# Causal attention over 32 keys in a perceiver kernel: values copied onto the diagonal of standing buffers, row sums as a column of ones, one key product, and both 32-key stages in written order

## The chip, the cores and the metric

The kernel runs on one core of one Trainium2 chip. The metric is the device time of one execution in microseconds. Five engines work side by side: PE (TensorE, matrix products), DVE (VectorE), ACT (ScalarE), POOL (GpSimd) and SP (SyncE, which issues transfers). Operands lie in SBUF, matrix products go to PSUM, which has eight banks of 512 float words for each of 128 partitions. PEld is the loading of PE's weights, which runs beside the products.

## The reference

The input x has 64 sequences of 32 tokens of 256 numbers; the context has 64 × 257 rows of 64 numbers. Six residual steps follow each other, each on a layer norm of x:

```python
x = x + _L0_xattn_ref(_layernorm(x), ctx_512, ...)   # A: 16 heads of 16, causal
x = x + _L0_attn_ref(_layernorm(x), ...)             # B: 16 heads of 128, shared key and value
x = x + _L0_ffn_ref(_layernorm(x), ...)              # C: the best 4 of 16 blocks
x = x + _L1_xattn_ref(_layernorm(x), ctx_512, ...)   # D: 16 heads over 257 rotated keys
x = x + _L1_attn_ref(_layernorm(x), ...)             # E: 16 heads of 16, causal, 4 key groups
x = x + _L1_ffn_ref(_layernorm(x), ...)              # F: 8 experts, the best one of them
```

The change is in A and E. The core of E (A is the same with 16 own key and value heads, without biases, and with an output product; only the first 32 of its keys are seen, since the mask is causal and there are 32 queries):

```python
q = jnp.einsum('bse,hed->bhsd', x, Wq) + bq[None, :, None, :]
kg = jnp.einsum('bse,ged->bgsd', x, Wk) + bk[None, :, None, :]
vg = jnp.einsum('bse,ged->bgsd', x, Wv) + bv[None, :, None, :]
k = jnp.repeat(kg, per, axis=1)      # each key group serves 4 heads
v = jnp.repeat(vg, per, axis=1)
scores = jnp.einsum('bhqd,bhkd->bhqk', q, k) * (1.0 / np.sqrt(d))
scores = jnp.where(causal[None, None, :, :], -jnp.inf, scores)
attn = jax.nn.softmax(scores, axis=-1)
out = jnp.einsum('bhqk,bhkd->bhqd', attn, v)
```

## The kernel before, in words

**Tiling.** The 2048 tokens are 16 tiles of 128 (four sequences of 32 each), which stay in SBUF as xs[t] for all six stages. Four tiles make a group: layer norms, their transposes (PE, then a copy by ACT) and the query and key products are made for a group of 512 tokens at a time; scores, softmax and outputs for a tile. The stages follow one another in one program: A (L335–487), B, C, D (to L1465), E (L1470–1703), F.

**A tile of a 32-key stage.** `scores` (L264) multiplies 32×32 blocks: 64 small matmuls give 16 heads of 32 queries × 32 keys for each of the four sequences, in a PSUM tile of four banks, of which the first 128 columns of each are used. `softmax_rows` (L211) is a chain over three engines: DVE scales and masks (L216), DVE takes the maximum (L225), POOL subtracts it (L226), ACT takes the exponential (L227), DVE sums (L229) and takes the reciprocal (L231). `heads_on_partitions` (L234) transposes the result on PE (L239) and ACT copies it to SBUF (L241), so that 4 heads × 32 keys lie on the partitions. `gather` multiplies by a block-diagonal matrix vd of the values: for each sequence j and each four heads c a matrix of 128 × 64, zero except where a row's head is the column's head.

**The values.** In A, `values` (L402) makes them with PE in two "mm" tiles (L410), and four DVE multiplications by the mask m4 write vd, zeros included (L420). In E, inside `score`, PE makes v in an "mm" tile (L1501), DVE adds the bias (vbe, L1509), and four POOL multiplications by m4 write vd (L1512), in a rotating set of three buffers. The "mm" tiles are two buffers that the transposes, the query and key products, the values and the router share.

**Normalising.** In A, POOL multiplies the exponentials by the reciprocal sums before the transpose (L399). In E, DVE multiplies the gathered output by them (L1532), and POOL adds it to x (L1538).

**The features of E.** `e_features` (L1158) makes q of a group (part 1; two column halves o) and the keys (part 2). For the keys, each half o is a product of its own (L1162) and two ACT steps with a 0/1 mask write kd (L1175), whose two halves hold the same keys.

**D's second half** also prepares E. A table of steps (L1349–1362), run one by one between D's products, holds for E the norms of groups 0 and 1 (steps 48 and 61), the start of group 0 (50), and its transposes, query and key products (51, 55, 56, 58, 59, 60).

**Routing in E.** F sends each token to one expert, so E also makes, as soon as tiles are done, their norm statistics (`route_stats`, DVE L152–153), the norm (`route_norm`: POOL copies L1551, the power on POOL, ACT L1558, more POOL copies), its transpose (`route_turn`, L1571, L1574), the router's product and argmax (`route`, L1583–1606, a chain of DVE steps that ends in oh and cum), and the ranks and the scattered rows (`send`, rank L1613, L1616, POOL's indirect transfers L1629). A table `routing` names the tile at which each runs: one group's four steps at t = 5–8, 9–12, 13–16, the last tiles' at 15 to 17.

**What sets the order.** The program's instructions are ordered for each engine by the framework's scheduler, except on the engines that a block lists in `manual_schedule(engines=...)`: there the written order stands. In A and in E only PE is listed. The loops of the two stages write it down:

```python
for t in range(NT + 2):                       # A, L470-487
    score(t + 1); project(t - 2); values(t + 1)
    turned[t] = heads_on_partitions(...); gather(t - 1)
    group(t // 4 + 1, t % 4)                  # norm and transposes of the next group at part 0
    for step in first.get(t, ()): step()      # B's first norms and keys, at t = 9 to 15
```

In E (L1680–1698) the order is score(t+1) with its values, heads of t, the features of the next group (for t > 1), gather(t−1), its route statistics, routing. In A the norm of the next group stands in part 0 of `group`, right ahead of its transposes; in E in part 3, a tile earlier.

Of the kernel before, what the change touches and what calls it, by code (L numbers as in the profile page):

```python
# [7 lines left out]
F32 = mybir.dt.float32  # L8
AF = mybir.ActivationFunctionType
ALU = mybir.AluOpType  # L10
# [35 lines left out]
def perceiver_kernel(ctx: ExitStack, tc: tile.TileContext, a: dict, out: bass.AP):  # L46
# [107 lines left out]

    def ln_group(g, name, twice=False, act=False, power=False):

        mv = sm(f"lnm_{name}{g}", [P, 4, 2])
        for i in range(4):
            stats(mv[:, i, :], xs[4 * g + i], f"{name}{g}_{i}")
        rs = rstd_of(mv, 4, f"{name}{g}", power)  # L160
        if twice:

            v2 = sm(f"lnw_{name}{g}", [P, 4, 2])
            nc.vector.tensor_tensor(v2[:, :, 1], mv[:, :, 1], rs, ALU.mult)
            nc.vector.tensor_tensor(v2[:, :, 1], v2[:, :, 1], rs, ALU.mult)
            rs2 = rstd_of(v2, 4, f"{name}{g}b", power)
            nc.vector.tensor_tensor(rs2, rs2, rs, ALU.mult)
            rs = rs2
        sh = sm(f"lnh_{name}{g}", [P, 4])
        nc.vector.scalar_tensor_tensor(sh, mv[:, :, 0], -1.0, rs, ALU.mult, ALU.mult)  # L170
        xn = []
        for i in range(4):
            y = xnp.tile([P, D], F32, tag="xn", name=f"xn_{name}{g}_{i}")
            x_ = xs[4 * g + i]
            if act:
                nc.scalar.activation(
                    y, x_, AF.Identity, scale=rs[:, i : i + 1], bias=sh[:, i : i + 1]
                )
            else:
                nc.vector.scalar_tensor_tensor(  # L180
                    y,
                    x_,
                    rs[:, i : i + 1],
                    sh[:, i : i + 1].to_broadcast([P, D]),
                    ALU.mult,
                    ALU.add,
                )
            xn.append(y)
        return xn
# [22 lines left out]
    def softmax_rows(s_ps, t, work, name):  # L212
# [14 lines left out]
        nc.scalar.activation(s, s, AF.Exp)  # L227
        su = sm(f"su_{name}{t}", [P, NH])
        nc.vector.tensor_reduce(su, s, AX.X, ALU.add)  # L229
        ri = sm(f"ri_{name}{t}", [P, NH])  # L230
        nc.vector.reciprocal(ri, su)  # L231
        return s, ri
# [31 lines left out]
    def scores(ps, qT, kd, i, name):  # L264

        s_ps = ps.tile([P, 4, 512], F32, tag="S", name=f"S_{name}")
        for o in range(KC):
            for j in range(4):
                for r in range(4):
# [4 lines left out]
                        kd[rs, o, 4 * i + j].rearrange("p w k -> p (w k)"),  # L274
# [61 lines left out]
    with tc.tile_pool(name="wA", bufs=2) as work, tc.tile_pool(  # L336
# [3 lines left out]
    ) as ps2, tc.manual_schedule(engines={mybir.EngineType.PE}):  # L340
# [15 lines left out]
        def group(g, part):  # L356
# [7 lines left out]
            if part == 0:  # L364
                feats[g][2] = transposed(ln_group(g, "a", power=True), ps2, g, "a")
# [27 lines left out]
        def score(t):  # L393
            g, i = divmod(t, 4)
            qT, kd, _ = feats[g]
            s_ps = scores(ps1, qT, kd, i, f"a{t}")
            sc[t] = softmax_rows(s_ps, t, work, "a")
            s, ri = sc[t]
# [57 lines left out]
        for _ in range(18):  # L456
            nc.tensor.matmul(warm, pad[:, 0:P], pad[:, 0:256], start=True, stop=True)
        for part in (0, 1, 2):
            group(0, part)
        score(0)  # L460
        values(0)

# [7 lines left out]
        for t in range(NT + 2):  # L470
# [8 lines left out]
            if t < NT:  # L479
                turned[t] = heads_on_partitions(sc.pop(t)[0], ps1, t, work, "a")  # L480
            if 1 <= t <= NT:
                gather(t - 1)
            group(t // 4 + 1, t % 4)
            for step in first.get(t, ()):
                step()
# [651 lines left out]
    with mbw, wd1:  # L1137
# [3 lines left out]
        with tc.tile_pool(name="wD", bufs=2) as work, tc.tile_pool(  # L1141
# [7 lines left out]

            def e_group_start(g):  # L1150
                feats[g] = (
                    e_w.tile([P, KC, 512], F32, tag="qT", name=f"qTe{g}"),
                    e_w.tile([P, KC, 16, 2, S], F32, tag="kd", name=f"kde{g}"),
# [3 lines left out]
            def e_features(g, part, o, ps):  # L1157

                qT, kd, xT = feats[g]
                q_ps = ps.tile([P, 512], F32, tag="mm", name=f"qe{g}_{o}_{part}")  # L1160
# [193 lines left out]
            steps[48] = lambda: lat.update(e=ln_group(0, "e", power=True))  # L1354
# [535 lines left out]
```

## Time and profile before

| what | value |
|---|---|
| runs | 1299.14, 1298.5 and 1304.86 us; median 1299.14 |
| the profiled execution's own time | 1298.15 us |
| its span, from first to last instruction | 1296.4 us |
| mean granted clock of PE, as a share of full | 0.943 |
| busy, share of the span: PE, DVE, ACT, POOL | 92%, 59%, 42%, 30% |
| instructions | 26028 |

The stages lie one after the other in the span: A to about 151 us, B and C after it, D from 660 to 992, E from 992 to about 1149, F to the end. Two windows of the trace, one of A and one of E, show what each engine did there. The columns are the window, its length, the busy time (and number of instructions) of PE, PEld, DVE, ACT and POOL, the granted clock, the share of the DMA engines in use, and GB/s:

```profile
18.00:145.00 127.00, 104.57 (x2194) 65.55 (x2196) 79.51 (x205) 51.98 (x102) 39.47 (x41) 0.89 0.66 208
1062.00:1072.00 10.00, 6.11 (x168) 5.05 (x168) 8.21 (x26) 1.64 (x4) 7.36 (x21) 0.57 0.01 2
```

In the views of groups, a line names the code line, the engine, the operation, output <- inputs and the shape of a kind of instruction, how often it ran, its busy time in us and the mean ns of one, and behind the last bar the idle time of its engine just before it and what ended it. A group can be busy for less than its number times its mean, since matmuls overlap. A releaser in square brackets in an order of time is the same for one instruction.

### The profile page before, as it was taken

What the parts mean: (1) busy time and instruction counts of PE and PEld (TensorE: products, weight loads), DVE (VectorE), ACT (ScalarE), POOL (GpSimd) and SP (SyncE); (2) the same over time, 40 slices, a digit from 0 to 9 for tenths busy, and PEclk for the clock granted to TensorE, in tenths of its full rate; (3) what the DMA queues carried; (4) which work ended last, traced back from release to release, by engine and by line L of the source; (5) the groups of instructions that cost most, each with busy time, mean ns of one, the idle gap of its engine ahead of it and who ended that gap; (6) DMA issues with size and microseconds to landing.
All of it is one profiled execution on the core that took longest, in us unless ns stands there. A gap on an engine that the chain in (4) does not pass through costs nothing. (4 is left out here: it accounts for less than half of the span.)

```text
span 1296.4 us, 26028 instructions
## 1 busy us (share of the span) xinstructions
PE 1187.8 (92%) x10189; PEld 833.3 (64%) x10189; DVE 769.0 (59%) x1751; ACT 540.1 (42%) x1255; POOL 389.7 (30%) x504
## 2 busy tenths in 40 slices
PE   6898999999999999999989999999998687669997
PEld 4555767767767566777756767777766455536664
DVE  5665345778758865533288877777674574334432
ACT  2336354554544641222365656556563233211111
POOL 2232251554524631000055252000002577621111
PEclk8889999999999989979999989999999788669999
DMA  7991110111021220912154353111103700011110
GB/s 232 309 332 36 28 42 1 41 42 41 25 83 42 59 65 2 283 33 68 44 149 131 62 143 93 46 35 48 34 1 127 266 3 19 22 50 42 43 39 18
DMA packets 94588, 103.10 MB, mean 80 GB/s; under 512 B 37664, under 2 KB 71201, under 8 KB 93986
## 3 DMA queue, kind: packets, MB, share of 16 engines
q1 hardware_dynamic: 92594, 97.19, 25.8%
q0 software_dynamic: 1872, 4.23, 0.9%
q8 instruction: 82, 1.34, 0.4%
q14 instruction: 40, 0.33, 0.1%
HBM read 69.45 MB, written 32.85 MB: 79 GB/s over the span
## 5 line engine op out<-in xcount | busy, mean ns | idle before, releaser
L1261 ACT ACTIVATE pp<-Sd,nm 128x257 f32<-128x257 f32 x256 | 118.2, 475 | 71.9 <-DVE nm L1257 66.1
L706 PE MATMUL qb<-xT_b,b_q 128*128 128x256 f32 x512 | 123.0, 389 | 0.0
L706 PEld LDWEIGHTS qb<-xT_b,b_q 128*128 128x128 f32 x512 | 95.6, 191 | 39.5 <-issue 19.6
L797 PE MATMUL yb<-b_o,oTb 128*128 128x256 f32 x512 | 116.1, 386 | 0.0
L797 PEld LDWEIGHTS yb<-b_o,oTb 128*128 128x128 f32 x512 | 98.4, 194 | 14.3 <-issue 1.0
L1270 DVE TENSOR_TENSOR pp<-pp,rd 128x514 f32<-128x514 f32 x128 | 98.4, 769 | 2.1
L1257 DVE TENSOR_REDUCE nm<-Sd 128x2 f32<-128x514 f32 x128 | 83.0, 685 | 19.2 <-PE Sd L1249 19.0
L1292 ACT COPY pTd<-pt 128x512 f32<-128x512 f32 x112 | 61.5, 599 | 52.1 <-PE pt L1286 52.1
L1309 PE MATMUL od<-pTd,na 128*64 128x256 f32 x480 | 66.3, 397 | 8.2 <-issue 6.5
L725 POOL TENSOR_TENSOR q2b<-qTb 128x512 f32<-128x512 f32 x64 | 65.2, 1048 | 27.0 <-ACT qTb L714 27.0
L1249 PE MATMUL Sd<-ct,qTd 64*128 64x257 f32 x480 | 69.2, 405 | 0.4 <-ACT pp L1261 0.2
L816 POOL TENSOR_TENSOR ynb<-ynb,vec 128x256 f32<-128x256 f32 x16 | 11.6, 726 | 191.3 <-DVE ynb L815 191.3
L714 ACT COPY qTb<-qb 128x512 f32<-128x512 f32 x64 | 37.5, 585 | 72.2 <-PE qb L706 70.6
L1286 PE MATMUL pt<-cst,pp 128*128 128x128 f32 x512 | 66.9, 274 | 0.0
L1286 PEld LDWEIGHTS pt<-cst,pp 128*128 128x128 f32 x512 | 59.0, 141 | 9.9 <-issue 5.6
L1068 PE MATMUL qd<-xT_d,d_m 128*128 128x256 f32 x256 | 64.4, 395 | 0.2 <-ACT xT_d L201 0.2
L759 DVE RECIPROCAL rqb<-rqb 128x512 f32<-128x512 f32 x16 | 53.5, 3344 | 17.8 <-ACT rqb L754 17.8
L588 PE MATMUL yc<-c,hc 128*128 128x256 f32 x256 | 59.4, 388 | 2.7 <-DVE hc L583 2.7
L1325 PE MATMUL yd<-d_n,co 128*128 128x256 f32 x256 | 61.5, 395 | 0.0
L1765 POOL DMA_INDIRECT out_dram<-os,ti x23 | 22.7, 986 | 124.4 <-DVE os L1762 100.8
L1068 PEld LDWEIGHTS qd<-xT_d,d_m 128*128 128x128 f32 x256 | 46.8, 192 | 17.0 <-issue 6.4
L773 DVE RECIPROCAL rdb<-denb 128x512 f32<-128x512 f32 x16 | 53.7, 3355 | 5.8 <-PE denb L771 5.6
(365 smaller groups left out, 2394.5 us busy)
## 6 DMA issues: line engine op xcount, KB each, us to landing
srt<-pad SPq DMA_DIRECT2D x17, 1040.0 KB
mb<-maskd SPq DMA_DIRECT2D x64, 128.0 KB
ct<-ctd SPq DMA_DIRECT2D x30, 257.0 KB
rct<-in_ctxT_dram SPq DMA_DIRECT2D x32, 128.5 KB
rrt<-in_ctxT_dram SPq DMA_DIRECT2D x64, 64.2 KB
ctd<-rct SPq DMA_DIRECT2D x32, 128.5 KB
nad<-rna SPq DMA_DIRECT2D x16, 256.0 KB
fw<-in_f_wg_dram SPq DMA_DIRECT2D x8, 512.0 KB
```

The costliest lines, as they stand in the source:

```text
L706: nc.tensor.matmul(q_ps[:, hh, :], b_q[:, k, h * P : (h + 1) * P], xT[:, k, c0 : c0 + 256], start=(k == 0), stop=(k == KC - 1),)
L725: nc.gpsimd.tensor_tensor(q2[:, 4 * h4 : 4 * h4 + 4, :], q, q, ALU.mult)
L797: nc.tensor.matmul(y_ps, oT[:, h, :], b_o[:, h, :], start=(h == 0), stop=(h == NH - 1))
L1068: nc.tensor.matmul(q_ps[:, r, :], m[:, k, pr * P : (pr + 1) * P], xT[:, k, c0 : c0 + 256], start=(k == 0), stop=(k == KC - 1),)
L1249: nc.tensor.matmul(s_ps[:, hh, :NKV], qT[hs, b % 8, 4 * u : 4 * u + 4, :], ct[hs, b % 4, :], start=True, stop=True,)
L1257: nc.vector.tensor_reduce(nm, s_ps[:, :, :NKV], AX.X, ALU.max, negate=True)
L1261: nc.scalar.activation(pp[:, hh, :], s_ps[:, hh, :NKV], AF.Exp, bias=nm[:, hh : hh + 1], accum_out=sd[:, hh : hh + 1],)
L1270: nc.vector.tensor_tensor(pp, pp, bc(rd, 2, NKV), ALU.mult)
L1286: nc.tensor.transpose(pt[:, hh * 256 + u * P : hh * 256 + u * P + P], probs[b][:, u, hh, c * P : (c + 1) * P], ident,)
L1292: nc.scalar.copy(pT[:, c, :], pt)
L1309: nc.tensor.matmul(o_ps[64 * hh : 64 * hh + 64, 0, :], na[:, j, c, :], pT[:, c, hh * 256 : (hh + 1) * 256], start=(c == 0), stop=(c == 1),)
L1325: nc.tensor.matmul(y_ps, co[:, pr, :], n[:, pr, :], start=(pr == 0), stop=False)
```

## The change

**Order.** In A the written order now holds on PE, DVE, ACT and POOL, in E on PE, DVE and ACT. The softmax is split so that its pieces can be placed: `softmax_rows` ends with POOL's subtraction, `power` is the exponential, and in A `share` is the sum, the reciprocal and POOL's multiplication. The layer norm is split as well (`ln_scale`, `ln_out`, which hold what `ln_group` held). In A the norm of the next group moves from part 0 to part 3 of `group` (t = 3, 7, and for group 1 ahead of the loop).

**E.** One PSUM tile of four banks, s_all, stands for the whole stage; scores go to columns 0–127 of each bank and the values of tile t to columns 128–383 of bank t mod 2, instead of an "mm" tile. Three value matrices vd also stand; they are zeroed once, in D's step 53, and get a 17th column for each head that holds the head mask m4. `place_values` then copies only the diagonal blocks, 32 partitions at a time: one by DVE, three by ACT. The gather has 68 columns for each four heads; the extra ones give the sums, so the reduction on DVE goes, and the reciprocal reads PSUM. The bias of the values is added to x instead (`e_bias`, four POOL additions for each group, in D for groups 0 and 1). The second key product goes: kd has one half, used for both. `route_norm` uses fewer POOL copies; `route_stats` stands last in a pass.

The diff, cut to its core:

```diff
+    def ln_scale(mv, name, twice=False, power=False):
...
+    def ln_out(x_, rs, sh, i, name, act=False):
...
@@ softmax_rows
         nc.gpsimd.tensor_tensor(s, s, bc(mx, 2, S), ALU.subtract)
-        nc.scalar.activation(s, s, AF.Exp)
-        su = sm(f"su_{name}{t}", [P, NH])
-        nc.vector.tensor_reduce(su, s, AX.X, ALU.add)
-        ri = sm(f"ri_{name}{t}", [P, NH])
-        nc.vector.reciprocal(ri, su)
-        return s, ri
+        return s
@@ scores
-                        kd[rs, o, 4 * i + j].rearrange("p w k -> p (w k)"),
+                        kd[rs, o % kd.shape[1], 4 * i + j].rearrange("p w k -> p (w k)"),
@@ A
-    ) as ps2, tc.manual_schedule(engines={mybir.EngineType.PE}):
+    ) as ps2, tc.manual_schedule(
+        engines={
+            mybir.EngineType.PE,
+            mybir.EngineType.DVE,
+            mybir.EngineType.Activation,
+            mybir.EngineType.Pool,
+        }
+    ):
...
             if part == 0:
-                feats[g][2] = transposed(ln_group(g, "a", power=True), ps2, g, "a")
+                feats[g][2] = transposed(lat.pop(g), ps2, g, "a")
+            if part == 3 and g + 1 < NG:
+                lat[g + 1] = ln_group(g + 1, "a", power=True)
...
+        def power(t):
+            nc.scalar.activation(sc[t], sc[t], AF.Exp)
+
+        def share(t):
+            s = sc[t]
+            su = sm(f"su_a{t}", [P, NH])
+            nc.vector.tensor_reduce(su, s, AX.X, ALU.add)
+            ri = sm(f"ri_a{t}", [P, NH])
+            nc.vector.reciprocal(ri, su)
             nc.gpsimd.tensor_tensor(s, s, bc(ri, 2, S), ALU.mult)
...
+        lat = {0: ln_group(0, "a", power=True)}
         for part in (0, 1, 2):
             group(0, part)
         score(0)
         values(0)
+        power(0)
+        lat[1] = ln_group(1, "a", power=True)
+        share(0)
...
+                turned[t] = heads_on_partitions(sc.pop(t), ps1, t, work, "a")
+            if t + 1 < NT:
+                power(t + 1)
             if 1 <= t <= NT:
                 gather(t - 1)
             group(t // 4 + 1, t % 4)
+            if t + 1 < NT:
+                share(t + 1)
@@ D
+            vd = [
+                e_w.tile([P, 4, 4, 4, NH + 1], F32, name=f"vde{z}", bufs=1) for z in range(3)
+            ]
+            def e_values():
+                for vd_ in vd:
+                    nc.gpsimd.memset(vd_, 0.0)
+                    nc.gpsimd.tensor_copy(
+                        vd_.rearrange("p j c h d -> p (j c) h d")[:, :, :, NH], bc(m4, 1, 16)
+                    )
+            def e_bias(g):
+                for t in range(4 * g, 4 * g + 4):
+                    x4 = xs[t].rearrange("p (c h d) -> p c h d", c=4, h=4)
+                    bv = vec[:, V_BV : V_BV + DC].rearrange("p (c d) -> p c d", c=4)
+                    nc.gpsimd.tensor_tensor(x4, x4, bc(bv, 2, 4), ALU.add)
...
+                if part == 2 and o > 0:
+                    return
...
+            steps[49] = lambda: e_bias(0)
+            steps[53] = e_values
+            steps[62] = lambda: e_bias(1)
-            for z, b_ in enumerate((51, 55, 56, 58, 59, 60)):
+            for z, b_ in enumerate((51, 55, 56, 58, 59)):
@@ E
+        s_all = ps1.tile([P, 4, 512], F32, name="S_e")
...
+        def norm(g, part):
+            if g >= NG:
+                return
+            if part == 0:
+                mvs[g] = sm(f"lnm_e{g}", [P, 4, 2])
+            if part < 2:
+                for i in (2 * part, 2 * part + 1):
+                    stats(mvs[g][:, i, :], xs[4 * g + i], f"e{g}_{i}")
+            if part == 1:
+                mvs[g] = ln_scale(mvs[g], f"e{g}", power=True)
+            if part == 2:
+                lat[g] = [ln_out(xs[4 * g + i], *mvs[g], i, f"e{g}") for i in range(4)]
+            if part == 3:
+                e_bias(g)
...
+        def values(t):
+            g, i = divmod(t, 4)
+            v_ps = s_all[:, t % 2, P : P + 4 * DC].rearrange("p (j d) -> p j d", j=4)
...
+        def place_values(t, v_ps):
+            for r in range(4):
+                rs = slice(32 * r, 32 * r + 32)
+                dst = vd[t % 3][rs].rearrange("p j c h d -> p (j c) h d")[:, :, r, :NH]
+                src = v_ps[rs].rearrange("p j (c d) -> p (j c) d", c=4)
+                if r == 0:
+                    nc.vector.tensor_copy(dst, src)
+                else:
+                    nc.scalar.copy(dst, src)
...
+            ri = sm(f"ri_e{t}", [P, NH])
+            nc.vector.reciprocal(ri, o_ps[:, :, NH])
...
+            if t + 1 < NT:
+                score(t + 1)
+            if t > 0:
+                gather(t - 1)
+            if t + 1 < NT:
+                v_ps[t + 1] = values(t + 1)
+            if t < NT:
+                turned[t] = heads_on_partitions(sc.pop(t), ps1, t, work, "e")
+            if t + 1 < NT:
+                power(t + 1)
             if t > 1:
                 group(t // 4 + 1, t % 4)
+            norm(t // 4 + 2, t % 4)
+            if t >= NT - 1:
                 route_stats(t - 1)
             for step, ts in routing.get(t, ()):
                 step(ts)
+            if t + 1 < NT:
+                place_values(t + 1, v_ps.pop(t + 1))
+            if 0 < t < NT - 1:
+                route_stats(t - 1)
```

## The prediction

> **What bounds the kernel now.** I read the page first, then the table by windows, the groups of the last attention stage, and its order of time.
>
> ```profile
> span 1296.4 us, 26028 instructions
> PE   6898999999999999999989999999998687669997
> PEclk8889999999999989979999989999999788669999
> ```
>
> TensorE is nearly full except in the first slices (stage A, up to 151 us) and in slices 32 to 36 (stage E, 992 to about 1149 us), where its clock is low too. Those two stages are what the change rewrites; C and F stay, B and D keep their bound (TensorE). The table by windows (us, then busy PE, PEld, DVE, ACT, POOL, then clock, DMA share, GB/s):
>
> ```profile
> 940.00:960.00 20.00, 19.61 (x135) 13.54 (x134) 14.78 (x37) 11.92 (x39) 0.00 (x0) 1.00 0.00 1
> 992.00:1128.00 136.00, 102.03 (x2777) 73.43 (x2776) 71.70 (x201) 44.05 (x78) 90.43 (x190) 0.81 0.29 103
> ```
>
> End of D: PE 98% busy, POOL empty. E: PE 75% at clock 0.81, and POOL with 90.43 us the next busiest. The groups of E (busy, mean ns | idle before, releaser):
>
> ```profile
> L1512 POOL TENSOR_TENSOR vde<-vbe,cst 128x256 f32<-128x256 f32 x64 | 37.9, 624 | 2.3 <-DVE vbe L1509 2.3
> L1501 PE MATMUL ve<-e_v,xT_e 128*32 128x64 f32 x1024 | 23.2, 253 | 8.5 <-issue 6.5 <-ACT qTe L1170 2.1
> L229 DVE TENSOR_REDUCE su_e<-s_e 128x16 f32<-128x512 f32 x16 | 10.9, 682 | 23.2 <-ACT s_e L227 23.2
> L1509 DVE TENSOR_TENSOR vbe<-ve,vec 128x256 f32<-128x256 f32 x16 | 6.7, 416 | 3.5 <-PE ve L1501 3.5
> L1613 PE MATMUL rank<-oh,tri 128*128 128x32 f32 (+2 forms) x10 | 2.8, 367 | 8.1 <-DVE oh L1601 8.1
> ```
>
> From the first scores (992.7) to the last gather (1119.7) E takes 127.1 us, of which the idle times ahead of PE's rows make 31 us. And one plain tile of E in order of time (start, duration):
>
> ```profile
> 1088.73 0.85 PE L271 MATMUL S_e<-kde,qTe 32*32 32x64 f32 x64
> 1089.52 1.10 PE L1501 MATMUL ve<-e_v,xT_e 128*32 128x64 f32 x64
> 1089.62 0.69 DVE L216 SCALAR_TENSOR_TENSOR s_e<-S_e,caus 128x512 f32<-128x512 f32 x1 [1.16 <-PE S_e L271]
> 1090.55 0.66 PE L239 MATMUL ptp_e<-cst,s_e 128*128 128x128 f32 x4
> 1091.21 1.05 POOL L226 TENSOR_TENSOR s_e<-s_e,mx_e 128x512 f32<-128x512 f32 x1 [2.49 <-PE ptp_e L239]
> 1091.30 0.59 ACT L241 COPY pT_e<-ptp_e 128x512 f32<-128x512 f32 x1 [1.87 <-PE ptp_e L239]
> 1092.29 0.63 ACT L227 ACTIVATE s_e<-s_e 128x512 f32<-128x512 f32 x1 [0.41 <-POOL s_e L226]
> ```
>
> The values follow the scores without a pause here, since they go into another buffer: the softmax of the next tile runs beside PE's work.
>
> **What the change takes out of E.** Per tile: four POOL multiplications (64 × 0.624 = 37.9 us in all, off PE's path except through vbe and the late x), the bias sum on DVE (16 × 0.416), the reduction for the sums (16 × 0.682), and one of two key products (half of the 12.4 us that 24 records of qe<-xT_e,e_k keep PE busy, and six of twelve masks at 0.77 on ACT). Taken alone that is worth much: PE's waits for vbe (6.8 us over its rows) and for oh, cum (about 5 of the 12 us: DVE's queue is shorter), the key product's 6.2 us, and some of the cold stretches. I put E without any new wait at 106 to 113 us, a gain of 14 to 21.
>
> **What it adds.** Scores and values now lie in one standing tile of four banks: the scores of a tile in columns 0 to 127 of all four, the values in columns 128 to 383 of bank 0 or 1. The trace has one case of two uses of one bank, od in D: the gather writes columns 0 to 255, the last key's product (L1222) is read by DVE at columns 256 and on.
>
> ```profile
> 719.45 0.68 DVE L1294 COPY pTd<-pt 128x512 f32<-128x512 f32 x1
> 720.05 0.28 DVE L1222 TENSOR_TENSOR lT<-od,maskj 128x128 f32<-128x128 f32 x1
> 720.44 0.63 PEld L1309 LDWEIGHTS od<-pTd,na 128*64 128x64 f32 x8 [0.33 <-issue]
> ```
>
> The gather's other input is there at 720.13; it starts only after lT's end at 720.33, and so in all 15 cases, with 0.045 us from lT's end to the release of PE. So a matmul waits for a read of another part of its bank. The Trainium skill ("PSUM — Partial Sum Buffer", section "PSUM bank collisions raise a hardware error") says the same: engines are to be kept apart by bank and quadrant of 32 partitions, not by address, so it speaks against values in the scores' banks; by its finer half, quadrants, nothing is saved here, since scores and copies both cover all four. If instead only addresses counted, the sum would be that of the gain above.
>
> Hence two waits that before does not have. First, the values of t+1 wait until DVE has read the scores of t+1. Second, the scores of t+2 wait for the four copies (one DVE, three ACT) that place the values of t+1. These stand last in the written order of both engines, behind the exponential, the features, norms and routing of the pass; PE has all that follows queued behind the scores. So a pass becomes a ring. By rows: scores to DVE 0.89, DVE 0.69, values 1.10 (the gather's 0.65 lies beside DVE), transposes to their copy 0.75, copy 0.59, exponential 0.63, three ACT copies. No row shows a 32-partition copy; the nearest, oTa (128x256, ACT, L443), takes 0.373, the floor is 0.19 (a two-column copy on POOL, L1551), the ceiling 0.59 (pT's 512 columns): I take 0.37, as its length per partition is the same, 1.11 for three (bounds 0.6 to 1.8). **A plain pass: 5.76 us** (5.2 to 6.4). Fifteen: 86.4.
>
> Work between the exponential and the copies, in ACT's order: copies of a group's transposes 2 × 0.59 (twice: 2.4); query products, 3.8 us of PE (11.5 us of qe<-xT_e,e_q for three groups) and the last ACT step of 0.68, less the 1.3 beside which PE already works: 3.1 (twice: 6.2); key product, 2.1 of PE and 2 × 0.77, less the same and some overlap: 2.1 (three: 6.3); xn_f 4 × 0.59 (three: 7.2); turned rows 2 × 0.60 (three: 3.6); router, 16 matmuls 2.17 and its DVE chain ahead of DVE's copy, 2.7 (twice: 5.4). Sum 31.1. The first tile, with two key products' preparation and no overlap, until the scores of 1: 11.2 (now 8.0; POOL's sixteen token copies, 0.19 and more each, stand before the exponential). The last gather 1.4. Together 86.4 + 31.1 + 11.2 + 1.4 = 130.1 at full clock, 3 more than now **with** its cold stretches.
>
> Cold stretches come on top. PE is at half clock in 1008.8–1019, 1029.3–1039.5, 1063.4–1073.7, 1094–1097.6, 1101–1107.8 and from 1118, five of the six beside a gap of 2.4 to 3.1 us without work; 1.6 us at 1078 did nothing. At half clock the values take 1.93 for 1.10, transposes 1.12 for 0.66, scores 1.10 for 0.85: 1.5 us more per pass, 2.5 to 3 with products. In the ring PE waits 2.4 us or more in each plain pass (5.76 less 0.89, 0.69, 1.10, 0.66). All 16 cold: +24; none: 0. Passes with products leave PE shorter gaps; I take the seven without: 7 × 1.5 = 10.5. The Trainium skill ("TensorE: Matmul & The Clock Gate", section "HAM oscillation — how this bites in real kernels") has a rule of no gaps above about 3.4 us; by it hardly a pass would be cold and the term near 0. The rows (2.4 us suffices) decide. Fetch stalls ("issue", 9.6 us over E's rows) were partly beside other waits; on a ring I add 5 (0 to 9). **E: 130.1 + 5 + 10.5 = 145.6, +18.5** (+3 to +36).
>
> **A.** PE loses waits for vda and its buffers (6.2 us over its rows), since DVE now takes the four multiplications straight after the values, and 2.5 at the start. But the norm of the next group (four statistics, POOL's two steps, the power at about 1.04 as L140, four scalings: 5.6 us on DVE) now stands ahead of the sums and POOL's share of tile t+1, at t = 3 and 7; PE's heads come 12.5 us after the scores, where PE is ready at 7.85: +4.6 each. keys_norm(0) does it once less (+1.5); colder stretches 0 to 3. −6.2 − 2.5 + 9.2 + 1.5 + 1.5 = **+3** (−6 to +9).
>
> **D and the end.** D loses one key product (12.4/6 = 2.1 us: −2.1); its new POOL work (three fills of 128x1088, eight bias sums of 0.73) lies where POOL is empty (156 us), costing PE nothing, 1 to 3 us if a fill is still running when E's first sub wants POOL. The tail loses POOL copies before the last rows' sends: −0.7 (−2 to 0). The other bias sums, eight more in E, fit in the 37.9 us freed.
>
> **Sum**, against the profiled execution (1298.15, span 1296.4): +18.5 + 3 − 2.1 − 0.7 = +18.7, 1316.9; the median of the runs stands 1.0 above that execution: **1318 us**. Bounds of this case 1302 to 1342, not all terms being at their ends at once.
>
> **Rivals.** (1) *The ring is not closed, faster.* If the copies are through before PE comes to the scores of t+2 (they take 0.2 each and run while PE gathers, or PE waits by address), POOL's 2.33 us per tile and the vbe waits go and E gains 14 to 21, A and D as above: about 1283 (1276 to 1291). For it: PE 75% busy, 31 us idle; against it: the 15 of 15 at od, and copies written last. It decides from a pass under 5.0 us and PE gaps under 2. Chance 0.27. (2) *A ring at full clock with hidden fetches:* no cold passes and a pass nearer 5.2 (15 × 0.56 = 8 less), E −5 to +3, about 1299, within 0.5%: 0.13. (3) *The forecast,* 1318: 0.45. (4) *Cold throughout:* every pass near 7.3 us, E +32 to +36, F's first tiles cold as well, 1332 to 1345: 0.15. That the change does not do what it says (a scheduler reorders the listed engines) is small here, since it fixes their order by hand; it would look like (2).
>
> The range reaches from the fast case to most of the cold one: 1279 to 1342. Within 0.5% (1292.6 to 1305.6) is about what a measurement here cannot tell from no change. Faster 0.27, same 0.13, slower 0.60; the likeliest case's own range is 1302 to 1342.
>
> **What would show it.** In E's order of time the scores' first weight load begins just after the last ACT copy of the values (right), or well after it or before (wrong); the values begin after DVE's reading of the scores; plain passes of 5.5 to 6 us, or 7 when cold; granted clock in 1000 to 1120 below 0.81; POOL under 50 us of 136; in A the heads of tiles 4 and 8 some 4 us late with DVE's norm ahead. Wrong if E's passes average under 7, or the gap ahead of each score is below 1 us.

## The result, and the profile after

The changed kernel takes 1339.49 us (median of four runs, 1336.82 to 1340.74), beside 1300.2 (median of four) for the kernel before: a ratio of 1.0294, with a 95% interval from 1.0261 to 1.0326. The forecast, 1318 us, had the sign and a little under half the size. The profiled execution took 1340.74 us. Its page:

```profile
span 1339.0 us, 25967 instructions
PE   7888999999999998999889999999996766559998
PEclk8887899999999999989989989999999767759999
```

The thin slices are still the first four and those of E (31 to 36), now thinner. Taking each stage from the last product of the one before to its own last product (E to the count of the routed rows), the span grew by 42.6 us like this:

| stage | before | after | difference | forecast |
|---|---|---|---|---|
| A | 151.0 | 168.0 | +17.0 | +3 |
| B and C | 492.8 | 492.1 | −0.7 | 0 |
| D | 347.9 | 353.7 | +5.8 | −2.1 |
| E | 150.1 | 172.2 | +22.1 | +18.5 − 0.7 |
| F | 154.5 | 153.0 | −1.5 | 0 |

D of the kernel before begins at 643.9 us of its span, right after C.

One profile is not a stage's last word. In the table below "E" goes from its first scores to its last gather, and each row is a profile. The last column is the median of the kernel's runs; the kernel before, run again beside the experiments, had medians of 1301.5 to 1303.8 us:

| run | A | B + C | D | E | F | median, us |
|---|---|---|---|---|---|---|
| before | 151.0 | 492.8 | 347.9 | 132.4 | 154.5 | 1300.2 |
| before_again | 154.3 | 488.6 | 348.3 | 130.4 | 154.3 | 1295.4 (one run) |
| changed kernel | 168.0 | 492.1 | 353.7 | 155.9 | 153.0 | 1339.5 |
| a_order_free | 142.0 | 494.8 | 357.2 | 163.6 | 153.2 | 1328.2 |
| a_norm_later | 162.7 | 491.9 | 352.3 | 164.0 | 153.2 | 1347.5 |
| a_norm_spread | 155.9 | 493.4 | 356.9 | 164.4 | 153.1 | 1339.5 |
| a_dve_free | 152.6 | 491.3 | 356.7 | 163.7 | 153.1 | 1333.5 |
| e_values_apart | 163.0 | 497.3 | 353.1 | 137.4 | 154.6 | 1319.1 |
| e_place_early | 159.8 | 494.6 | 349.5 | 137.7 | 154.0 | 1320.8 |
| e_act_copies_early | 162.0 | 495.3 | 350.9 | 143.8 | 154.4 | 1326.3 |
| e_dve_copy_early | 165.6 | 494.7 | 352.7 | 147.1 | 153.1 | 1330.8 |
| e_keep_warm | 163.0 | 497.3 | 356.5 | 149.8 | 153.4 | 1334.7 |
| all_order_free | 145.6 | 501.4 | 354.0 | 129.6 | 154.5 | 1293.4 |
| a_free_e_apart_early | 144.4 | 488.6 | 352.5 | 137.9 | 154.4 | 1298.5 |
| a_free_e_apart_free | 147.4 | 501.4 | 352.1 | 129.5 | 154.2 | 1296.9 |
| all_free_warm | 142.9 | 494.5 | 354.8 | 142.8 | 154.3 | 1307.2 |
| d_fills_late | 146.2 | 491.5 | 349.7 | 125.9 | 153.0 | 1291.4 |

So A's text as in the changed kernel took 159.8 to 168.0 us (six profiles), its E 155.9 to 164.4 (five): the profile of the changed kernel is at the long end of the one and the short end of the other.

**E is the ring.** A plain pass of the changed kernel in order of time:

```profile
1025.63 0.85 PE L270 MATMUL S_e<-kde,qTe 32*32 32x64 f32 x64 [1.94 <-ACT vde L1596]
1026.60 0.69 DVE L221 SCALAR_TENSOR_TENSOR s_e<-S_e,caus 128x512 f32<-128x512 f32 x1 [8.53 <-PE S_e L270]
1027.35 1.10 PE L1578 MATMUL S_e<-e_v,xT_e 128*32 128x64 f32 x64 [0.86 <-DVE s_e L221]
1028.38 0.66 PE L239 MATMUL ptp_e<-cst,s_e 128*128 128x128 f32 x4
1029.07 0.59 ACT L241 COPY pT_e<-ptp_e 128x512 f32<-128x512 f32 x1 [3.49 <-PE ptp_e L239]
1029.55 0.63 ACT L1570 ACTIVATE s_e<-s_e 128x512 f32<-128x512 f32 x1
1030.21 1.15 ACT L1596 COPY vde<-S_e 32x256 f32<-32x256 f32 x3
1031.41 0.98 PE L270 MATMUL S_e<-kde,qTe 32*32 32x64 f32 x64 [2.38 <-ACT vde L1596]
```

From scores to scores it is 5.78 us (forecast 5.76), the three copies 1.15 (forecast 1.11), and the next scores start 0.05 us after the last copy's end, here and in all 15 passes. The values (L1578) wait for DVE's reading of the scores. It is the only pass at full clock: the other three without a group's products or routing took 7.10 to 7.47 us, with values of 1.93 to 2.39 us instead of 1.10, about the 7.26 that the forecast has for a cold pass. PE's waits in E:

```profile
PE S_e L270 <- ACT vde L1596: 47.7, 15, 6.0
```

47.7 us in 15 places, where the kernel before had none. But the long passes are longer than forecast. This is the pass t = 6 of the loop, from the scores of tile 7 to those of tile 8:

```profile
1082.83 0.66 PE L1652 MATMUL tpf<-cst,xn_f 128*128 128x128 f32 x4 [1.10 <-ACT kde L1223]
1083.19 2.61 DVE L178 SCALAR_TENSOR_TENSOR xn_e<-x,lnr_e,lnh_e 128x256 f32<-128x256 f32 x4 [5.55 <-PE tpf L1652]
1085.72 0.41 DVE L1594 COPY vde<-S_e 32x256 f32<-32x256 f32 x1
1086.16 1.15 ACT L1596 COPY vde<-S_e 32x256 f32<-32x256 f32 x3 [2.06 <-DVE vde L1594]
1087.37 1.10 PE L270 MATMUL S_e<-kde,qTe 32*32 32x64 f32 x64 [3.88 <-ACT vde L1596]
```

DVE's norm scalings wait for PE's transposes to give their buffers back; DVE's copy stands behind them, and ACT's three wait for DVE's. The pass is 12.97 us; the forecast's pieces give 9.06 (5.76, 2.1 for the key product, 1.2 for the turned rows).

**A has a long queue on DVE, and a low clock behind it.** Around tile 8, with the norm of the next group in one piece:

```profile
94.64 0.85 PE L270 MATMUL S_a<-kda,qTa 32*32 32x64 f32 x64
95.87 0.39 DVE L152 BATCH_NORM_STATS2 lnb_a<-x 128x6 f32<-128x256 f32 x1
96.88 1.04 POOL L140 TENSOR_TENSOR lnr_a<-lnr_a,mhalf 128x4 f32<-128x4 f32 x1
98.15 1.67 DVE L178 SCALAR_TENSOR_TENSOR xn_a<-x,lnr_a,lnh_a 128x256 f32<-128x256 f32 x4
99.74 0.68 DVE L414 TENSOR_REDUCE su_a<-s_a 128x16 f32<-128x512 f32 x1
100.85 1.05 POOL L417 TENSOR_TENSOR s_a<-s_a,ri_a 128x512 f32<-128x512 f32 x1 [2.93 <-DVE ri_a L416]
101.95 1.12 PE L239 MATMUL ptp_a<-cst,s_a 128*128 128x128 f32 x4 [4.37 <-POOL s_a L417]
```

This is the wait that was forecast (4.6; here 4.37), and PE comes out of it at half clock (1.12 for 0.66). At the start of A PE is at half clock from the first heads on: they come at 30.15, behind 5.47 us of waiting for POOL's share, which stands behind the norm of group 1, and take 1.11 us. Then one wait for a late instruction ("issue": nothing that the profile shows) is added, and the query products behind it are still slow:

```profile
38.20 0.76 PE L428 MATMUL va<-a_kv,ctxa 64*32 64x256 f32 x11 [2.61 <-issue]
41.78 5.50 PE L380 MATMUL qa<-xT_a,a_q 128*128 128x512 f32 x8
```

The same eight records of query products took 3.67 us before. Over the whole stage the clock is the larger loss (kernel before, then the changed kernel; columns as in the table by windows above):

```profile
18.00:151.00 133.00, 110.57 (x2271) 70.59 (x2272) 80.62 (x207) 53.24 (x104) 39.47 (x41) 0.90 0.63 199
18.00:168.00 150.00, 122.46 (x2271) 80.01 (x2272) 82.90 (x216) 55.23 (x106) 39.89 (x42) 0.81 0.56 176
```

The same 2271 products took 11.9 us more at clock 0.81 instead of 0.90; PE's idle time grew by some 5 us.

### The profile page after: what moved, and what is told of

It is laid out like the page before. It is cut to its first block, busy times and chain, and to the rows that moved or that the text cites. A ratio compares the mean times of both kernels' runs of the same rounds, so it can differ in the third digit from the quotient of the medians.

```text
span 1339.0 us, 25967 instructions
## 1 busy us (share of the span) xinstructions
PE 1197.5 (89%) x10173; PEld 848.3 (63%) x10173; DVE 767.7 (57%) x1740; ACT 554.5 (41%) x1297; POOL 363.7 (27%) x430
## 5 line engine op out<-in xcount | busy, mean ns | idle before, releaser
L1305 DVE TENSOR_REDUCE nm<-Sd 128x2 f32<-128x514 f32 x128 | 82.9, 684 | 20.0 <-PE Sd L1297 19.9
L270 PE MATMUL S_e<-kde,qTe 32*32 32x64 f32 x1024 | 16.1, 268 | 48.2 <-ACT vde L1596 47.7
L1373 PEld LDWEIGHTS yd<-d_n,co 128*128 128x128 f32 x256 | 49.8, 200 | 13.0 <-issue 6.1
```

Source lines behind the costliest of these rows:

```text
L1305: nc.vector.tensor_reduce(nm, s_ps[:, :, :NKV], AX.X, ALU.max, negate=True)
L1373: nc.tensor.matmul(y_ps, co[:, pr, :], n[:, pr, :], start=(pr == 0), stop=False)
```

## The experiments

**a_order_free.** A's order:

```diff
-        engines={
-            mybir.EngineType.PE,
-            mybir.EngineType.DVE,
-            mybir.EngineType.Activation,
-            mybir.EngineType.Pool,
-        }
+        engines={mybir.EngineType.PE}
```

> The changed kernel, but in stage A only PE keeps the written order; DVE, ACT and POOL are ordered by the scheduler again. Theory (the 17 us that A lost come from the written order of these three, the next group's norm ahead of the sums above all): A ends near 152 us of the span instead of 168, the whole near 1323 us. Rival (A lost them on PE itself, to late instructions and a low clock that come with the new text whatever the order): A still ends near 168, the whole near 1339.

A ended at 142.0, 10 us earlier than expected and 9 earlier than in the kernel before. The theory holds, the rival falls: on the same products the written order of the other three engines costs A some 19 us (163.6, the mean of the six profiles with A's written order unaltered, against 144.8, the mean of the six with it free), and the rest of A's edits gain 8 (before: 151.0 and 154.3). The low clock goes with the order: with it free, PE's products from 18 us to the end of A took 107.6 to 110.5 us in these six profiles.

The time came to 1328.18 only: in the profile E was 7.7 us longer than in the changed kernel's, D 3.5, B and C 2.7. In E two passes (t = 9 and 13) make 6.4 us of it. There the scores or the gather came in pieces of about five records with a wait for issue between them, as here in pass 9:

```profile
1092.62 0.47 PE L1596 MATMUL oe<-vde,pT_e 128*32 128x68 f32 x5 [0.30 <-issue]
```

and DVE's scaling began 5.4 us after its scores, against 1.2 in the changed kernel. All four kernels here that have A's text changed and E's not (E 163.6 to 164.4) have both stretches, the changed kernel's profile (155.9) neither; what brings them stays open.

**a_norm_later.**

```diff
-            if part == 3 and g + 1 < NG:
-                lat[g + 1] = ln_group(g + 1, "a", power=True)
...
                 share(t + 1)
+            if t % 4 == 3 and t // 4 + 2 < NG:
+                lat[t // 4 + 2] = ln_group(t // 4 + 2, "a", power=True)
```

> The changed kernel, with the norm of the next group in A moved behind the sums and the share of the next tile (at t = 3 and 7, and ahead of the loop). Theory (these norms stand ahead of the share and hold back PE's transposes, 13.5 us of waits of the transposes for POOL in three places): A ends 8 to 11 us earlier, the whole near 1330. Rival (the next tile's scaling and maximum on DVE are then held back as long): A unchanged within 2 us, 1339.

A 162.7: inside the range of the unmoved ones, and the whole time rose to 1347.5. From heads to heads, tiles 4 and 8 fell from 9.2 and 9.1 to 5.6 and 4.5 us, and tiles 5 and 9 rose from 7.1 and 9.1 to 12.1 and 13.3. The rival was right: moved as one piece, the norm holds the next pass.

**a_norm_spread.** With a `norm(g, part)` in four parts as E has it:

```diff
-            if part == 3 and g + 1 < NG:
-                lat[g + 1] = ln_group(g + 1, "a", power=True)
...
                 share(t + 1)
+            norm(t // 4 + 2, t % 4)
```

> The changed kernel; in A the norms of groups 2 and 3, which stand in one piece ahead of the share of tiles 4 and 8, are cut into four parts, one in each pass and each behind the share, so that DVE never waits for POOL's power (two statistics; two statistics and the power; two scalings; two scalings). The written order on all four engines stays. Theory (a norm in one piece of 5.6 us on DVE's queue, with the wait for POOL in it, is what holds a pass, wherever it stands): the passes of tiles 4 and 8, 9.2 us from heads to heads, fall to 5.5 to 6.5, and A ends 5 to 8 us earlier than the 160 to 168 us of the three runs with the same A, near 157. Rival (what counts is the amount of DVE work in the order): the passes that take the parts get longer and A ends at 160 to 168.

Tiles 4 and 8: 7.6 and 4.5 us instead of 9.2 and 9.1, the tiles behind them 5.5 and 6.9 instead of 7.1 and 9.1, and tile 10 0.8 longer; A 155.9, near the 157 expected. The theory is right, tile 4 half of it. The whole time did not move (1339.53), with E at 164.4 and D at 356.9 in the profile.

**a_dve_free.**

```diff
             mybir.EngineType.PE,
-            mybir.EngineType.DVE,
             mybir.EngineType.Activation,
```

> The changed kernel; in A PE, ACT and POOL keep the written order and only DVE is ordered by the scheduler. Theory (A's loss is DVE's written order: norms in one piece, the keys' norm, multiplications of the values straight behind the maximum): A ends at 142 to 148 us, as with all three engines free, the whole near 1322. Rival (ACT's or POOL's order is a cause too): A ends at 152 to 165.

A 152.6 is just inside the rival's range, and halfway between the means of the free and the written order (144.8 and 163.6): DVE's order is a large part, not all. Tile 8 was still 8.0 us, and the first two passes took 19.3 together, with the late instruction, against 13.6 in a_order_free. Which part is ACT's, which POOL's and which the late instruction's is not shown.

**e_values_apart.**

```diff
-            v_ps = s_all[:, t % 2, P : P + 4 * DC].rearrange("p (j d) -> p j d", j=4)
+            v_ps = ps2.tile([P, 4, DC], F32, tag="mm", name=f"ve{t}")
```

> The changed kernel, but the values of E go into a shared two-buffer tile of their own bank, as before the change; the copies to the diagonal and all orders stay. Theory (the scores wait for the copies because they share banks: 47.7 us of waits of PE for ACT in 15 places): these waits fall to under 10 us, E from the first scores to the last gather goes from 156 to 125 to 135 us, the whole near 1314. Rival (the written order of ACT and DVE holds E, and the bank only names the wait): E shortens by under 8 us, the whole over 1331.

E 137.4, a little over the range expected, and the wait of the scores for the copies is gone from PE's list, which now begins:

```profile
PE ve L1578 <- issue: 7.2, 8, 3.5
PE tp_e L214 <- ACT xT_e L215: 6.4, 3, 2.8
```

The scores began 1.1 to 10.3 us before the last copy's end in every pass. Sharing is a cause: without it the same written order costs 18 to 27 us less in E. Whether it goes by the bank or by the tile is not shown: s_all is one tile of four banks, and this edit takes the values out of both. In the changed kernel the first of the 64 score products goes to bank 0, and it waited 0.05 us beyond the last copy even where the values lay in bank 1; that one product speaks for the tile.

**e_place_early.**

```diff
                 power(t + 1)
+                place_values(t + 1, v_ps.pop(t + 1))
...
-            if t + 1 < NT:
-                place_values(t + 1, v_ps.pop(t + 1))
             if 0 < t < NT - 1:
```

> The changed kernel, with the four copies of a tile's values placed right behind its exponential, ahead of the group's features, the norm and the routing on ACT and DVE. Theory of the ring (the copies' place in the order sets the pass): the passes with a group or routing shrink by the 1.2 to 5.5 us of ACT's work and E by 15 to 25 us, the whole near 1319; plain passes stay near 5.8 us. Rival (the work that the copies pass is late next and holds PE all the same): E unchanged within 5 us.

E 137.7, 18 us less than in the changed kernel's profile: the place in the order is a cause as well, and as large. With the copies early, the wait for them is 15.8 us in 9 places.

**e_act_copies_early, e_dve_copy_early.** `place_values` takes a list of copies; the first kernel as below, the second with (0,) and (1, 2, 3) exchanged:

```diff
                 power(t + 1)
+                place_values(t + 1, v_ps[t + 1], (1, 2, 3))
...
-                place_values(t + 1, v_ps.pop(t + 1))
+                place_values(t + 1, v_ps.pop(t + 1), (0,))
```

> The changed kernel; of the four copies of a tile's values the three on ACT stand right behind the exponential, DVE's one stays last. Theory of the forecast (ACT's work ahead of its copies makes the ring long): E falls from 156 to 164 us to 137 to 145, as with all four early. Rival (DVE's copy, behind the norm's scalings, which wait for PE's transposes, and behind the router's chain, is what closes the long passes): E stays at 150 to 164, with PE's scores waiting for DVE's copy instead of ACT's.

> The changed kernel; of the four copies only DVE's one stands right behind the exponential's place, ahead of the norm and the routing on DVE; ACT's three stay last. Theory of the forecast (ACT's order): E stays at 150 to 164 us. Rival (DVE's copy closes the long passes): the passes of tiles 6 to 11, 10 to 13.5 us from heads to heads, fall by 2 to 4 us each, E to 140 to 150. If both engines' orders hold the ring in turn, each of the two kernels gives a part and the parts add to the 18 to 26 us of the early copies on both.

E 143.8 and 147.1. Against the changed kernel's own profile (155.9), which like these two has no stretch of late instructions as in a_order_free, that is 12.1 and 8.8 less, 20.9 together; both early gave 18.2, so the parts about add. Against the mean of the five profiles with all four copies last (162.3) they would overlap (18.5, 15.2 and 24.6); the spread of E does not let one decide. In the first, PE waits for the other engine:

```profile
PE S_e L270 <- DVE vde L1594: 29.6, 11, 3.9
```

Both orders hold the ring in turn. The forecast's theory of ACT alone is out, and so is that of DVE alone. In the second, pass 6 fell from 13.0 to 10.8 us from heads to heads and pass 7 from 12.5 to 8.4.

**e_keep_warm.** Behind the routing of each pass:

```diff
+            if t + 2 < NT:
+                idle = ps2.tile([P, 256], F32, tag="mm", name=f"idle{t}")
+                for _ in range(5):
+                    nc.tensor.matmul(idle, pad[:, 0:P], pad[:, 0:256], start=True, stop=True)
```

> The changed kernel, with five products more in each pass of E, of zeros into a shared tile that nobody reads, put on PE behind the routing and ahead of the next scores, where PE waits for the copies. They add work (about 1.9 us per pass at full clock) and take none away. Theory (PE's gaps of 2.4 us and more keep its clock low in E, and the low clock lengthens the ring): the values go back from 1.94 to 1.10 us, the transposes from 1.12 to 0.66, and E from the first scores to the last gather from 156 to 164 us to 140 to 148. Rival (the clock is not what these passes wait for, or the added products stand in the way): E unchanged or up to 10 us longer.

E 149.8, with the granted clock there 0.93 instead of 0.77. PE's groups in E:

```profile
L1791 PE MATMUL idle<-pad 128*128 128x256 f32 x140 | 34.8, 398 | 2.0 <-ACT qTe L1218 1.1 <-ACT xT_e L215 0.9
L1578 PE MATMUL S_e<-e_v,xT_e 128*32 128x64 f32 x1024 | 22.4, 249 | 6.2 <-DVE s_e L221 5.2 <-issue 1.0
```

PE did 34.8 us more, and the values took 22.4 instead of 28.4 us. E is 6.1 us shorter than in the changed kernel's own profile and 12.5 than the mean of the five, and just over the range expected: the low clock is a part of the ring's length. The forecast had 10.5 for it.

**all_order_free.** The edit of a_order_free, and in E:

```diff
             mybir.EngineType.PE,
-            mybir.EngineType.DVE,
-            mybir.EngineType.Activation,
```

> The changed kernel with only PE in written order, in A and in E, as before the change; the layout of the values, the copies, the sums as a column and the one key product stay. Theory (two causes in E, the bank that scores and values share and the place of the copies in the written order; the scheduler can put the copies early): E from 156 to 164 us to 132 to 145, A near 142, the whole near 1305. Rival (with the shared bank the order hardly matters, the ring stays closed): E over 150 us, the whole over 1318.

1293.43 us, a ratio of 0.9918 (0.9883 to 0.9953): 0.8% shorter than the kernel before, and 46 us shorter than the changed kernel. E 129.6, with the bank still shared and 20.7 us of waits for the copies in ten places. The rival falls: with the tile still shared, the order decides.

**a_free_e_apart_early, a_free_e_apart_free.** The edits of a_order_free and e_values_apart together, in the first with that of e_place_early, in the second with E's of all_order_free.

> The changed kernel with three things taken back or moved: A's DVE, ACT and POOL ordered by the scheduler, the values of E in a tile of their own bank, and their copies right behind the exponential. If the three losses found add up (A 168 to 142 us, E 156 to 137 by the banks, and some of the 18 us that the early copies gave where the banks are not in the way), the time is 1280 to 1292, below the kernel before. If the two edits in E cure the same wait, the second adds nothing: 1292 to 1298. If a new wait takes their place (PE's features or POOL's subtraction), over 1300.

> As the kernel before it in this list, but with DVE and ACT of E ordered by the scheduler too, in place of copies put early by hand: the change's layout without the shared bank and without its written orders. If the written order of E is a loss by itself, E is shorter than with the copies put early by hand and the time below 1285; if it is of use once the copies are early, E is 3 to 10 us longer.

The first: 1298.53, 0.9978 (0.9944 to 1.0012), no difference; E 137.9. The two edits cure the same wait (137.4, 137.7, both 137.9). The second: E 129.5, shorter than with the copies put early by hand, and 1296.91 us, 0.9957 (0.9921 to 0.9993), not the time below 1285 that was set for it. Once DVE and ACT are ordered freely, parting the banks adds nothing (129.6 and 129.5).

**all_free_warm.** The edits of all_order_free, and those of e_keep_warm with `range(4)`.

> The kernel with only PE in written order in both stages (E 129.6 us), with four products of zeros more at the end of each pass of E, as before in the changed kernel. If the low clock is still worth more than the 1.5 us of added products per pass, E falls to 118 to 126 us and the time below 1290; if the passes no longer have gaps to fill, the products stand in the way: E 130 to 145.

E 142.8 at clock 0.92: 13 us longer, as the second case has it. PE was busy for 116.6 us of E instead of 92.5. That the added products stand in the way is argued, not shown: this profile also has a 6.3 us wait of DVE in front of one scaling, as in a_order_free, which all_order_free's has not.

**d_fills_late.** The fills made dependent on D's step 48:

```diff
-                    nc.gpsimd.memset(vd_, 0.0)
+                    flat = vd_.rearrange("p j c h d -> p (j c h d)")
+                    nc.gpsimd.tensor_copy(flat, late.to_broadcast([P, 16 * 4 * (NH + 1)]))
```

> The kernel with only PE in written order in both stages; the three standing buffers are filled by a copy on POOL from a column of zeros that is made from a norm output of E's first group (xn times 0), so that the fills can't run before D's step 48. Theory (the fills at D's start, 4 us of POOL where it turns the keys, delay D): D falls from 349 to 357 us to 346 to 350 and the whole by 4 to 6 us, near 1288. Rival (D is longer for another reason, such as late instructions: 9 to 12 us of waits for issue ahead of one line, against 6.5 and 6.9 before): D stays at 352 to 357.

The fills ran at 861 us, D took 349.7, and the whole 1291.35: 0.9913 (0.9888 to 0.9938), the shortest of all. But e_place_early had D at 349.5 with the fills at its start, so the 4.3 us of D to all_order_free's profile are not shown to be the fills'.

**before_again.**

> The kernel before once more, for a second profile of it. Stages that no edit touches (B, C, most of D, F) took 995 to 1010 us together in the ten profiles so far, 995 in the one of the kernel before. If this spread is one between executions, the second profile lies somewhere in that range; if the kernel before has an advantage there, it is at 995 again.

B, C, D and F together: 991.2, against 995.2 in the first profile, and so under the range. In the fifteen profiles with the change or a part of it, the same stages took 994.2 to 1009.9, D alone 349.5 to 357.2 against 347.9 and 348.3. D was longer in all fifteen; the cause stays open.

## Why the prediction fell short

The sign and the mechanism of E were right: the two waits, the order of the ring, a plain pass of 5.76 us (5.78 at full clock), the first tile's 11.2 (10.9), copies at 0.37 each (0.38), waits of the scores for ACT's last copy. The rival of an open ring would have needed either the copies early or the values in a tile of their own: both were made here, and each took E back to 137. Even so neither reaches its 106 to 113 us; the best E is 125.9. That figure took off waits as if no others would take their place; with the values apart PE waits 7.2 us for issue and 6.4 for ACT's copies of xT_e.

In the profile the sum missed by 24 us: A by 14.0 (17.0 for 3), D by 7.9, E with its tail by 4.3, less 0.7 in B and C and 1.5 in F. These terms were mis-sized or misread.

**"A: −6.2 − 2.5 + 9.2 + 1.5 + 1.5 = +3"** (it adds to 3.5). The waits were about right. The heads of tile 8 waited 4.37 us where 4.6 was forecast, the first heads came 2.6 us earlier (30.15 for 32.77), and PE's waits for vda fell from 5.3 us to 0.5. The term that failed is "colder stretches 0 to 3", put at 1.5: the same products took 11.9 us more in the changed kernel's profile. So the first two passes took 19.9 us instead of 13.4, with the half clock and the late instruction shown above; e_place_early, with the same A and no such late instruction, had 13.6. And the keys' norm, +1.5, cost 4 to 6: the pass to tile 11 was 13.7 us, for 7.7 in a_order_free and 9.3 in d_fills_late. There the keys' norms of two groups run on DVE and ACT ahead of the next tile's scaling and exponential. That of group 0 is in A's written order; that of group 1 stands at the head of B's text (L847), and the scheduler ran it among A's instructions. The two square roots come apart, with an exponential between them, so ACT loads its table seven times in A instead of five, at 1.28 us each. A range of −6 to +9 did not hold +17; the mean of six profiles against two is +11.

**"From the first scores (992.7) to the last gather (1119.7) E takes 127.1".** The gather at 1119.7 is the one before the last; the last one starts at 1124.3, and E takes 132.4. The forecast of E, 145.6, was 10.3 us under the 155.9 measured. Its difference, +18.5 for 23.5, looks closer only because the base was 5.3 too short as well, which is luck. In the mean of five profiles against two, E grew by 31 us (162.3 against 131.4).

**"Work between the exponential and the copies, in ACT's order … 31.1".** Only ACT's queue was summed. In the long passes DVE's copy stands behind norm scalings that wait for PE's transposes, or behind the router's chain, and ACT's copies wait for DVE's. So passes 6 and 7 took 13.0 and 12.5 us where the forecast's pieces give 9.1 and 8.5. In e_keep_warm, at clock 0.93, they were 11.2 and 11.0 (from scores to scores), so a part of this is the clock, which the forecast counted in seven passes only.

**"Fetch stalls … on a ring I add 5".** PE's waits for issue in E were 1.0 us in the changed kernel's profile. In the four others with the same E text they were 3.6 to 4.4, and the two passes with late instructions took 3.4 and 2.9 us longer. The term fits these four, not the one profile.

**"D … its new POOL work … lies where POOL is empty (156 us), costing PE nothing".** D was forecast at −2.1 and took +5.8. The fills did not run at the end of D: they stand in step 53 of the text, but only PE is in written order in D, and the profile shows them released by C's last products:

```profile
L1183 POOL MEMSET vde<- x3: 1007/1008/1026, 660.7 to 662.7; 128x1088 f32 x3
671.45 1.27 POOL L667 TENSOR_TENSOR rct<-rct,cst 128x514 f32<-128x514 f32 x1 [6.14 <-issue]
```

POOL was empty there too: it had been idle for 122 us, and it was idle again for 6.1 us before it turned the first keys (second line). So nothing shows that the fills cost D its time. The bias sums ran at 885 and 968 us, also behind idle time. PE's waits for issue ahead of the gather's line in D were 9.0 to 12.1 us in eight profiles with the change or a part of it, 6.5 and 6.9 before; that is the measured companion of D's longer time, not its shown cause, which stays open.

The part of the Trainium skill on banks ("PSUM — Partial Sum Buffer", section "PSUM bank collisions raise a hardware error") agrees with the runs as far as they go: the scores waited for copies of other columns of their banks (47.7 us in 15 places), and with the values in another bank they did not. Since the values then lay in another tile too, no run here parts the two. The rule on gaps ("TensorE: Matmul & The Clock Gate", section "HAM oscillation — how this bites in real kernels") was rightly set aside for the rows: seven of the ring's waits were 2.38 to 2.70 us long, and behind each the values of the pass took 1.51 to 2.67 us instead of 1.10.

## What to carry to other kernels

Where one engine's writes share a PSUM tile with another's reads, look at what stands in every reader's queue ahead of its last read, and follow every copy's own waits; one engine's sum is a lower bound. Before the order of an engine is fixed by hand, check each long piece in it (a norm with a round trip to another engine) against what is queued behind: cut into parts it cost little at tile 8 (4.5 us from heads to heads) and some 3 us at tile 4 (7.6), in one piece 4 to 5 us wherever it stood. And price the clock with the waits: in A it cost more than they did. The same edits without the written orders on DVE, ACT and POOL beat the kernel before by 0.8% (all_order_free, 1293.43 us), with the fills late by 0.9% (1291.35).

## What the runs showed of the hardware that was not expected

PE's clock can be low without an idle PE. In C of the changed kernel (columns as in the table by windows above):

```profile
585.00:600.00 15.00, 15.00 (x80) 14.37 (x80) 5.93 (x23) 0.80 (x2) 0.00 (x0) 0.66 0.01 1
```

By the profile's records, in which the ends of products are modelled, PE is busy for all 15 us at clock 0.66; 11.2 us of its work there are 64 products of 96x64 (t2p). In the kernel before the same stretch has 0.66 too. C, which no edit touches, took 131.6 to 141.4 us in four profiles, with more such stretches in the longest (0.83, 0.63 and 0.81 in all_order_free).

Work added to PE can shorten a stage that is bound by a ring (e_keep_warm, 34.8 us more of products, E 6 to 12 us shorter); in all_free_warm E was 13 us longer with it.
